# A state-space loop redistributed over the engines: the product with B on GpSimd, the decay in PSUM, the sum over states by accumulating transposes

## The chip, the cores and the metric

The kernel runs on one core of a Trainium2 chip. A core has TensorE (matrix products, PE in the profile; its weight loads are the row PEld), VectorE (DVE), ScalarE (ACT), GpSimd (POOL) and SyncE (SP), which here only issues transfers. They run side by side and wait for each other by semaphores. SBUF is the working memory, PSUM the memory that TensorE writes to; PSUM has eight banks, each of 512 fp32 values per partition. The metric is device time in microseconds for one execution of the whole program, the median of several.

## The reference

The program is two layers of a sequence model with many parts (a conditioned scan, attention, two feed-forward networks, a recurrent network, a mixture of experts). The change touches one part alone, a selective state-space model over 64 sequences of 64 steps and width 256. Its input is the output of the recurrent network. Cut to what matters:

```python
xz = x @ W_in                                # 256 -> 2 * 512
xi, z = jnp.split(xz, 2, axis=-1)
xc = silu(conv4(xi) + b_conv)                # causal, 4 taps, each channel by itself
delta_lr, B, C = jnp.split(xc @ W_xproj, [r, r + n], axis=-1)   # r = 16, n = 16
delta = softplus(delta_lr @ W_dt + b_dt)     # 512 channels
A = -jnp.exp(A_log)                          # 512 x 16
dA  = jnp.exp(delta[..., None] * A)          # decay
dBx = delta[..., None] * B[:, :, None, :] * xc[..., None]
def step(h, inp):                            # along the 64 steps of a sequence
    h = dA_t * h + dBx_t                     # 512 channels x 16 states
    y = einsum('bdn,bn->bd', h, C_t) + D * x_t
    return h, y
...
return y * silu(z) @ W_out
```

For each of the 16 states n the kernel does the same four things with an array of channels by time: an exponential (dA), a product with B's row n, a scan along time, and a product with C's row n. The results are summed over n.

## The kernel before

The 4096 tokens go in 8 chunks of 512 (CH), each 8 whole sequences. The 512 inner channels are four blocks (NI = 4) of 128 partitions. head(c) prepares a chunk in pieces that are interleaved with the states of the chunk before. PSUM is a pool of four banks called ps and four called acc for the whole program. The order in which each engine's instructions stand is set when the program is built.

```python
dAs = [p1.tile([P, NI, CB, L + 1], F32, name=f"dA{i}") for i in range(2)]
hbs = [p1.tile([P, NI, CB, L + 1], F32, name=f"hb{i}") for i in range(3)]
...                                   # column 0 of each sequence is zero, so that the scan restarts
def head(c, v):
    for i in range(NI):
        ps = bank(g)
        for k in range(KD):                                          # L579
            nc.tensor.matmul(ps, w.Win[:, k, ts(i, P)], hs2[:, k, tok], ...)
        acc = v.xc[:, i, :]
        nc.scalar.activation(acc, ps, AF.Identity, bias=..., scale=...)   # L581
        for s in range(1, 4):                                        # L584
            nc.vector.scalar_tensor_tensor(to, seq(ps)[...], taps, to, ALU.mult, ALU.add)
        yield
    nc.scalar.activation(v.xc, v.xc, AF.Silu)
    ...                                   # sz = silu(z): 4 x (two products, one Silu), L592, L593
    ...                                   # dbc = xc @ W_xproj (48 rows: delta_lr, B, C), L597, L598
    for i in range(NI):
        ps = bank(g)
        nc.tensor.matmul(ps, w.Wdt[:, ts(i, P)], v.dbc[:R, :], start=True, stop=True)   # L602
        nc.scalar.activation(z, ps, AF.Identity, bias=...)
        softplus(nc, z, ...)              # 3 on ScalarE, 4 on VectorE (L63 to L69)
        nc.vector.tensor_mul(v.dx[:, i, :], z, v.xc[:, i, :])        # L606
        yield

def broadcast(v, n):                      # rows B_n and C_n onto all 128 partitions
    got = []
    for row in (R + n, R + S + n):
        ps = bank(g)
        nc.tensor.matmul(ps, g.ident[:W, row:row+1].to_broadcast([W, P]), v.dbc, ...)   # L614
        got.append(...)
    return got
...
for c in range(NCH):
    yp = [bank(g, tag="acc") for _ in range(NI)]
    for n in range(S):
        dA, hb = dAs[n % 2], hbs[(c * S + n) % 3]
        for i in range(NI):
            nc.scalar.activation(dA[:, i, :, 1:], seq(now.delta[:, i, :]), AF.Exp, scale=w.A[:, i, n:n+1])  # L629
        nc.vector.tensor_tensor(hv, dx, bc[0], ALU.mult)                        # L634
        nc.vector.tensor_tensor_scan(hf, dA, hf, 0.0, ALU.mult, ALU.add)        # L635
        nc.vector.tensor_tensor(hv, hv, bc[1], ALU.mult)                        # L636
        if n + 1 < S:
            bc = broadcast(now, n + 1)
        for i in range(NI):
            nc.tensor.matmul(yp[i], g.ident, hb[:, i, :, 1:], start=(n == 0), stop=(n == S - 1))   # L640
        next(pieces, None)
    ...
    for i in range(NI):
        nc.vector.scalar_tensor_tensor(xc[:, i, :], xc[:, i, :], D, yp[i], ALU.mult, ALU.add)   # L648
        nc.gpsimd.tensor_mul(xc[:, i, :], xc[:, i, :], now.sz[:, i, :])         # L651
    for k in range(KD):                   # W_out: 4 products each (L655), added to xT (L657)
        ...
```

The scan is one instruction over 4 blocks x 8 sequences x 65 = 2080 elements per partition. The sum over states is four fp32 products with the identity per state (L640), which add up in PSUM. An fp32 product has two records in the trace.

Of the kernel before, what the change touches and what calls it, by code (L numbers as in the profile page):

```python
# [11 lines left out]
F32 = mybir.dt.float32  # L12
BF16 = mybir.dt.bfloat16
AF = mybir.ActivationFunctionType
# [4 lines left out]
P = 128  # L19
# [14 lines left out]
def setup(ctx, tc, a):  # L34

    nc = tc.nc
    g = SimpleNamespace(nc=nc, tc=tc, a=a)
    const = ctx.enter_context(tc.tile_pool(name="const", bufs=1))
    g.psum = ctx.enter_context(tc.tile_pool(name="psum", bufs=4, space=PSUM))
    g.ident = const.tile([P, P], F32, name="ident")  # L40
    make_identity(nc, g.ident)
    g.identb = const.tile([P, P], BF16, name="identb")
    make_identity(nc, g.identb)
    g.xT = const.tile([P, KD, NT], F32, name="xT")
    for k in range(KD):
        nc.sync.dma_start(g.xT[:, k, :], a["xT"][ts(k, P), :])
    g.condT = const.tile([P, KD, B], F32, name="condT")
    nc.sync.dma_start(g.condT, a["condT"].rearrange("(k p) b -> p k b", p=P))
    return g


def bank(g, shape=(P, CH), dt=F32, tag="ps"):
# [500 lines left out]
def mamba(g, w, hs):  # L553
    nc, tc = g.nc, g.tc
    NI, S, R = w.NI, w.S, w.R
    W = R + 2 * S
    nc.scalar.activation(w.A, w.A, AF.Exp)
    nc.vector.tensor_scalar(w.A, w.A, -1.0, None, ALU.mult)
    hs2 = hs.rearrange("p k b t -> p k (b t)")
    seq = lambda t: t.rearrange("p (b l) -> p b l", l=L)  # L560
    with tc.tile_pool(name="m1", bufs=1) as p1, tc.tile_pool(name="m2", bufs=2) as p2:

        dAs = [p1.tile([P, NI, CB, L + 1], F32, name=f"dA{i}") for i in range(2)]
        hbs = [p1.tile([P, NI, CB, L + 1], F32, name=f"hb{i}") for i in range(3)]
        for t in (*dAs, *hbs):
            nc.gpsimd.memset(t[:, :, :, 0:1], 0.0)

        def head(c, v):

            tok = ts(c, CH)  # L570
            v.xc = p2.tile([P, NI, CH], F32, name="xc")
            v.sz = p2.tile([P, NI, CH], F32, name="sz")
            v.delta = p2.tile([P, NI, CH], F32, name="delta")
            v.dx = p2.tile([P, NI, CH], F32, name="dx")
            v.dbc = p2.tile([W, CH], F32, name="dbc")
            for i in range(NI):
                ps = bank(g)
                for k in range(KD):
                    nc.tensor.matmul(ps, w.Win[:, k, ts(i, P)], hs2[:, k, tok], start=(k == 0), stop=(k == KD - 1))  # L579
                acc = v.xc[:, i, :]  # L580
                nc.scalar.activation(acc, ps, AF.Identity, bias=w.col[:, 0, i : i + 1], scale=w.taps[:, i, 3:4])  # L581
                for s in range(1, 4):
                    to = seq(acc)[:, :, s:]
                    nc.vector.scalar_tensor_tensor(  # L584
                        to, seq(ps)[:, :, : L - s], w.taps[:, i, 3 - s : 4 - s], to, ALU.mult, ALU.add
                    )
                yield
            nc.scalar.activation(v.xc, v.xc, AF.Silu)
            for i in range(NI):
                ps = bank(g)  # L590
                for k in range(KD):
                    nc.tensor.matmul(ps, w.Win[:, k, ts(NI + i, P)], hs2[:, k, tok], start=(k == 0), stop=(k == KD - 1))  # L592
                nc.scalar.activation(v.sz[:, i, :], ps, AF.Silu)  # L593
            yield
            ps = bank(g)
            for i in range(NI):
                nc.tensor.matmul(ps[:W, :], w.Wxp[:, i, :], v.xc[:, i, :], start=(i == 0), stop=(i == NI - 1))  # L597
            nc.scalar.copy(v.dbc, ps[:W, :])  # L598
            yield
            for i in range(NI):  # L600
                ps = bank(g)
                nc.tensor.matmul(ps, w.Wdt[:, ts(i, P)], v.dbc[:R, :], start=True, stop=True)  # L602
                z = v.delta[:, i, :]
                nc.scalar.activation(z, ps, AF.Identity, bias=w.col[:, 1, i : i + 1])  # L604
                softplus(nc, z, p2.tile([P, CH], F32, name="t1"), p2.tile([P, CH], F32, name="t2"))
                nc.vector.tensor_mul(v.dx[:, i, :], z, v.xc[:, i, :])  # L606
                yield

        def broadcast(v, n):

            got = []
            for row in (R + n, R + S + n):
                ps = bank(g)
                nc.tensor.matmul(ps, g.ident[:W, row : row + 1].to_broadcast([W, P]), v.dbc, start=True, stop=True)  # L614
                got.append(seq(ps).unsqueeze(1).to_broadcast([P, NI, CB, L]))
            return got

        now = SimpleNamespace()
        for _ in head(0, now):
            pass  # L620
        bc = broadcast(now, 0)
        for c in range(NCH):
            after = SimpleNamespace()
            pieces = head(c + 1, after) if c + 1 < NCH else iter(())
            yp = [bank(g, tag="acc") for _ in range(NI)]
            for n in range(S):
                dA, hb = dAs[n % 2], hbs[(c * S + n) % 3]
                for i in range(NI):
                    nc.scalar.activation(  # L629
                        dA[:, i, :, 1:], seq(now.delta[:, i, :]), AF.Exp, scale=w.A[:, i, n : n + 1]  # L630
                    )
                hv = hb[:, :, :, 1:]
                hf = hb.rearrange("p i b l -> p (i b l)")
                nc.vector.tensor_tensor(hv, now.dx.rearrange("p i (b l) -> p i b l", l=L), bc[0], ALU.mult)  # L634
                nc.vector.tensor_tensor_scan(hf, dA.rearrange("p i b l -> p (i b l)"), hf, 0.0, ALU.mult, ALU.add)  # L635
                nc.vector.tensor_tensor(hv, hv, bc[1], ALU.mult)  # L636
                if n + 1 < S:
                    bc = broadcast(now, n + 1)
                for i in range(NI):
                    nc.tensor.matmul(yp[i], g.ident, hb[:, i, :, 1:], start=(n == 0), stop=(n == S - 1))  # L640
                next(pieces, None)
            for _ in pieces:
                pass
            if c + 1 < NCH:
                bc = broadcast(after, 0)
            xc = now.xc
            for i in range(NI):
                nc.vector.scalar_tensor_tensor(  # L648
                    xc[:, i, :], xc[:, i, :], w.col[:, 2, i : i + 1], yp[i], ALU.mult, ALU.add
                )  # L650
                nc.gpsimd.tensor_mul(xc[:, i, :], xc[:, i, :], now.sz[:, i, :])  # L651
            for k in range(KD):
                ps = bank(g)
                for i in range(NI):
                    nc.tensor.matmul(ps, w.Wout[:, i, ts(k, P)], xc[:, i, :], start=(i == 0), stop=(i == NI - 1))  # L655
                x = g.xT[:, k, ts(c, CH)]
                nc.vector.tensor_add(x, x, ps)  # L657
            now = after
# [446 lines left out]
@with_exitstack  # L1105
def tile_adaln_attn_ffn_d2(ctx: ExitStack, tc: tile.TileContext, a: dict, out: bass.AP):
    g = setup(ctx, tc, a)
    p_mamba, close_mamba = scoped(tc, "w_mamba")
    p_mid, close_mid = scoped(tc, "w_mid")
    p_attn, close_attn = scoped(tc, "w_attn")  # L1110

    w_scan = scan_weights(g, p_attn)
    cs = conditioned_scan(g, w_scan, p_attn)
    w_attn = attention_weights(g, p_attn)
    w_ffn0 = ffn0_weights(g, p_mid)
    w_rnn = rnn_weights(g, p_mid)
    w_mamba = mamba_weights(g, p_mamba)
    rows = regions(g, p_mamba, "ffn1")
    attention(g, w_scan, w_attn, cs)
    close_attn()  # L1120

    ffn0(g, w_ffn0)

    p_hs, close_hs = scoped(tc, "hs", side="right")
    hs = p_hs.tile([P, KD, B, L], F32, name="hs")
    rnn(g, w_rnn, hs)
    close_mid()
    mamba(g, w_mamba, hs)
    close_hs()
    close_mamba()  # L1130

    x2 = ctx.enter_context(tc.tile_pool(name="x2", bufs=1))
    x2T = x2.tile([P, KD, NT], F32, name="x2T")
    routed = ctx.enter_context(tc.tile_pool(name="routed", bufs=1))
    gate = Gate(g, routed, x2T, rows)
    p_moe, close_moe = scoped(tc, "w_moe")
    with tc.tile_pool(name="gate2", bufs=2) as work:
        moe(g, moe_weights(g, p_moe), x2T, lambda c: gate.chunk(c, work))
    close_moe()
    ffn1(g, gate, out)  # L1140


# [76 lines left out]
```

## Time and profile before

| | |
|---|---|
| time, median of 3 | 4410.67 us (4409.87 to 4413.94) |
| span of the profiled execution | 4399.1 us |
| busy PE / VectorE / ScalarE / GpSimd | 3609.5 / 2209.0 / 1187.3 / 195.5 us |
| state-space stage | 1220.6 to 2693.5 us |
| VectorE busy from 1220.6 to 2692 | 1321 of 1471 us |
| largest shares of the chain that ended last | DVE hb L635 10%; PE ps L1044 8%; PE ps L894 8% |

In the page's costliest groups a row reads: line, engine, operation, output <- inputs with partitions x elements, count, then the busy time, the mean of one in ns, and after the second bar the time that the engine was idle just before, with what ended most of that idle time. The granted clock is the share of TensorE's full clock. Several records can overlap, so sums of records can be over the time that they took.

### The profile page before, as it was taken

Reading aid. Unit: us, or ns where it says so; the run is one execution under the profiler, and the core shown is the slowest. Engines: PE = TensorE matmul, PEld = TensorE weight load, DVE = VectorE, ACT = ScalarE, POOL = GpSimd, SP = SyncE. Lnnn points to the kernel's source line nnn. Section 1 sums busy time; section 2 is a strip of 40 time slices with the busy share of each in tenths; the row PEclk is TensorE's granted clock in tenths of the full one; section 3 lists DMA queues with packets and bytes.
Section 4 is the critical chain, followed back from the end, with each engine's and each line's share of the span. In section 5 each row is a group of like instructions: output and inputs, shape, how many; then the busy total and the mean of one; then the engine's idle time right before and its main releaser. Section 6 shows DMA issues by size and latency. Waiting matters only on the chain.

```text
span 4399.1 us, 34313 instructions
## 1 busy us (share of the span) xinstructions
PE 3609.5 (82%) x13521; PEld 1996.3 (45%) x13521; DVE 2209.0 (50%) x2286; ACT 1187.3 (27%) x1967; POOL 195.5 (4%) x247
## 2 busy tenths in 40 slices
PE   3799974549977878778778778999999994999993
PEld 3344432329932322223223225444444444888882
DVE  0355557770069889998898994211111121222223
ACT  0422214432245334244343420111111110111110
POOL 0000000000000000000000000000000001000005
PEclk9899986765578878878788786999999997999995
DMA  9940000000000000000000001000000004555543
GB/s 248 386 169 1 1 1 0 1 0 1 1 0 0 0 0 0 0 0 0 0 0 0 0 0 68 0 4 10 9 10 10 9 9 153 168 171 171 168 141 120
DMA packets 192785, 223.36 MB, mean 51 GB/s; under 512 B 35296, under 2 KB 162080, under 8 KB 192112
## 3 DMA queue, kind: packets, MB, share of 16 engines
q1 hardware_dynamic: 183360, 194.16, 13.9%
q0 software_dynamic: 9264, 27.01, 1.8%
q8 instruction: 106, 1.74, 0.2%
q14 instruction: 55, 0.45, 0.0%
HBM read 131.22 MB, written 89.92 MB: 50 GB/s over the span
## 4 chain that ended last, share of the span: by engine, by line
PE 60%; DVE 27%; issue 5%; ACT 3%; DMA 2%; POOL 1%; SPq 1%; DVEq 0%; POOLq 0%; ACTq 0%
DVE hb L635 10%; PE ps L1044 8%; PE ps L894 8%; PE acc L912 7%; DVE hb L634 5%; PE acc L1065 5%; DVE hb L636 5%; PE acc L279 3%; PE ps L899 3%; PE acc L299 3%; PE acc L640 2%; PE ps L263 2%; PE acc L292 1%; PE acc L827 1%; PE ps L521 1%
## 5 line engine op out<-in xcount | busy, mean ns | idle before, releaser
L640 PE MATMUL acc<-hb,ident 128*128 128x512 f32 x1024 | 630.1, 774 | 254.0 <-DVE hb L636 253.6
L635 DVE TENSOR_TENSOR_SCAN hb<-dA,hb 128x2080 f32<-128x2080 f32 x128 | 572.1, 4482 | 4.2
L640 PEld LDWEIGHTS acc<-hb,ident 128*128 128x128 f32 x1024 | 245.3, 251 | 646.9 <-DVE hb L636 330.6
L629 ACT ACTIVATE dA<-delta,A 128x512 f32<-128x512 f32 x512 | 333.3, 711 | 656.3 <-DVE hb L635 655.6
L1044 PE MATMUL ps<-gxT,w 128*128 128x256 f32 x1560 | 348.5, 383 | 0.9 <-issue 0.9
L1049 DVE TENSOR_TENSOR gh<-gs,ps 128x256 f32<-128x256 f32 x195 | 82.1, 421 | 473.3 <-ACT gs L1048 473.3
L1044 PEld LDWEIGHTS ps<-gxT,w 128*128 128x128 f32 x1560 | 294.2, 191 | 52.5 <-issue 13.8
L614 PE MATMUL ps<-dbc,ident 48*128 48x512 f32 x512 | 271.8, 648 | 51.9 <-ACT delta L604 29.6
L634 DVE TENSOR_TENSOR hb<-dx,ps 128x2048 f32<-128x2048 f32 x128 | 290.2, 2280 | 21.8 <-PE ps L614 21.7
L906 DVE TENSOR_TENSOR h<-act,acc 128x512 f32<-128x512 f32 x128 | 88.0, 688 | 412.7 <-ACT act L903 211.3
L636 DVE TENSOR_TENSOR hb<-hb,ps 128x2048 f32<-128x2048 f32 x128 | 290.3, 2279 | 5.1
L894 PE MATMUL ps<-xT,moe_r 128*128 128x512 f32 x512 | 240.6, 592 | 0.0
L912 PE MATMUL acc<-h,moe_r 128*128 128x512 f32 x512 | 239.4, 592 | 0.0
L1065 PE MATMUL acc<-w,gh 128*128 128x256 f32 x936 | 231.3, 392 | 0.0
L903 ACT ACTIVATE act<-ps 128x512 f32<-128x512 f32 x128 | 76.4, 597 | 423.5 <-PE ps L894 423.5
L1065 PEld LDWEIGHTS acc<-w,gh 128*128 128x128 f32 x936 | 165.0, 189 | 55.0 <-issue 38.8
L614 PEld LDWEIGHTS ps<-dbc,ident 48*128 48x128 f32 x512 | 87.5, 193 | 220.6 <-issue 137.7
L584 DVE SCALAR_TENSOR_TENSOR xc<-ps,taps,xc 128x504 f32<-128x504 f32 (+2 forms) x96 | 68.3, 723 | 226.2 <-ACT xc L581 226.0
L901 DVE SCALAR_TENSOR_TENSOR h<-ps,act 128x512 f32<-128x512 f32 x64 | 44.2, 691 | 256.8 <-PE ps L899 256.8
L1048 ACT ACTIVATE gs<-ps 128x256 f32<-128x256 f32 x195 | 74.9, 384 | 320.6 <-PE ps L1044 320.6
L894 PEld LDWEIGHTS ps<-xT,moe_r 128*128 128x128 f32 x512 | 97.3, 190 | 122.4 <-issue 122.4
L469 PE MATMUL ps<-identb,q 128*128 128x128 bf16 x256 | 27.9, 275 | 149.6 <-DVE q L412 149.6
(309 smaller groups left out, 4818.2 us busy)
## 6 DMA issues: line engine op xcount, KB each, us to landing
w<-in_ffn_W_dram SPq DMA_DIRECT2D x117, 640.0 KB, 4.7
ffn_x<-zero SPq DMA_DIRECT2D x32, 1024.0 KB, 10.7
ffn_y<-zero SPq DMA_DIRECT2D x32, 1024.0 KB, 10.7
gx<-ffn_x SPq DMA_DIRECT2D x39, 256.0 KB, 4.5
ffn_y<-gy POOLq DMA_DIRECT2D x39, 256.0 KB, 4.5
w<-in_ffn_W_dram SPq DMA_DIRECT2D x117, 64.0 KB, 4.3
xT<-in_xT_dram SPq DMA_DIRECT2D x2, 2048.0 KB, 10.5
T<-in_cond_pad_dram SPq DMA_DIRECT2D x2, 2048.0 KB, 22.1
```

What stands on the lines that cost most here:

```text
L279: nc.tensor.matmul(ps, y[:, k, ts(pr, P)], wa.Wv[:, k, ts(hg, 8 * V)], start=(k == 0), stop=(k == KD - 1))
L299: nc.tensor.matmul(ps, wa.Wout[:, i, ts(k, P)], oT[:, i, :], start=(i == 0), stop=(i == H // 2 - 1))
L614: nc.tensor.matmul(ps, g.ident[:W, row : row + 1].to_broadcast([W, P]), v.dbc, start=True, stop=True)
L629: nc.scalar.activation(dA[:, i, :, 1:], seq(now.delta[:, i, :]), AF.Exp, scale=w.A[:, i, n : n + 1])
L634: nc.vector.tensor_tensor(hv, now.dx.rearrange("p i (b l) -> p i b l", l=L), bc[0], ALU.mult)
L635: nc.vector.tensor_tensor_scan(hf, dA.rearrange("p i b l -> p (i b l)"), hf, 0.0, ALU.mult, ALU.add)
L636: nc.vector.tensor_tensor(hv, hv, bc[1], ALU.mult)
L640: nc.tensor.matmul(yp[i], g.ident, hb[:, i, :, 1:], start=(n == 0), stop=(n == S - 1))
L894: nc.tensor.matmul(ps, lhs[:, k, ts(j, P)], x[:, k, :], start=(k == 0), stop=(k == KD - 1))
L912: nc.tensor.matmul(po[k], lhs[:, j, ts(k, P)], h, start=(i == 0), stop=(i == total - 1))
L1044: nc.tensor.matmul(ps[:, j, :], v.w12[:, k, ts(j * full + i, P)], v.xT[:, k, :], start=(k == 0), stop=(k == KD - 1))
L1065: nc.tensor.matmul(po[:, s, :], v.h[r, i, ts(s, P)], v.w3[r, i, :], start=(i == 0), stop=(i == full))
```

## The change

Work is moved off VectorE. The product with B (L634) goes to GpSimd[...]; so B's rows are no longer spread by TensorE but written to DRAM and read back with a partition broadcast, four states at a time. The decay dA moves from SBUF to PSUM, so that the scan reads only one operand from SBUF. C's rows are still spread by TensorE, but in bf16: each fp32 value is split into three bf16 parts, which lie at partitions 0, 32 and 64 of one tile, and one bf16 product with a selecting column adds them up. The sum over states is no longer a product with the identity as the weights but a transpose, which adds up in PSUM with hb as the weights; what it sums is transposed, so it is copied to SBUF and transposed back once per half chunk. As the eight PSUM banks now hold dA (4), the sums (2), C (1) and all other products (1), a step handles two of the four channel blocks, and a chunk is two rounds of 16 states. Two of the softplus' operations go to GpSimd, and the softplus' ScalarE operations are batched by function. The general PSUM pool is closed before the stage and opened again after it. The core of the diff, with cuts marked:

```diff
-    with tc.tile_pool(name="m1", bufs=1) as p1, tc.tile_pool(name="m2", bufs=2) as p2:
-        dAs = [p1.tile([P, NI, CB, L + 1], F32, name=f"dA{i}") for i in range(2)]
-        hbs = [p1.tile([P, NI, CB, L + 1], F32, name=f"hb{i}") for i in range(3)]
+        tc.tile_pool(name="m3", bufs=3) as p3,
+        tc.tile_pool(name="mps", bufs=1, space=PSUM) as pp,
+    ):
+        one = lambda: pp.tile([P, CH], F32, name="mp")
+        dAs = [pp.tile([P, PI, CB, L], F32, name=f"dA{i}") for i in range(2)]
...
+        rows = 2 * 32 + S
+        parts = [p1.tile([rows, CH], BF16, name=f"parts{i}") for i in range(2)]
...
             for i in range(NI):
-                ps = bank(g)
+                ps = one()
...                                         # the same for every product of the head
+            v.B = tc.dram_tile((S, CH), F32, name=f"B{c}")
+            nc.sync.dma_start(v.B, v.dbc[R : R + S, :])
...                                         # C in three bf16 parts: 3 copies on ScalarE, 2 subtractions on VectorE
-                softplus(nc, z, p2.tile([P, CH], F32, name="t1"), p2.tile([P, CH], F32, name="t2"))
-                nc.vector.tensor_mul(v.dx[:, i, :], z, v.xc[:, i, :])
...                                         # Abs, one Exp and one Ln over all four blocks; 3 on VectorE per block
+                nc.gpsimd.tensor_sub(z, z, v.dx[:, i, :])
+                nc.gpsimd.tensor_mul(v.dx[:, i, :], z, v.xc[:, i, :])
...
+        def spread_b(v, n):
+            t = p3.tile([P, NB, CH], F32, name="Bn")            # NB = 4
+            nc.sync.dma_start(t, v.B[n : n + NB, :].partition_broadcast(P))
+            return t
...
-            yp = [bank(g, tag="acc") for _ in range(NI)]
-            for n in range(S):
+            for i0 in range(0, NI, PI):                          # PI = 2
+                yp = [pp.tile([P, CH // P, P], F32, name=f"yp{i}") for i in range(PI)]
+                for n in range(S):
+                    if n % NB == 0:
+                        Bn = spread_b(now, n)
+                    dA = dAs[step % 2]
...
+                    hb = p3.tile([P, PI, CH], F32, name="hb")
+                    nc.gpsimd.tensor_mul(hb, now.dx[:, i0 : i0 + PI, :], Bn[:, n % NB, :]...)
+                    cb = pp.tile([P, CH], F32, name="cb")
+                    nc.tensor.matmul(cb, pick[:, n : n + 1].to_broadcast([rows, P]), now.parts, start=True, stop=True)
-                nc.vector.tensor_tensor(hv, now.dx.rearrange("p i (b l) -> p i b l", l=L), bc[0], ALU.mult)
-                nc.vector.tensor_tensor_scan(hf, dA.rearrange("p i b l -> p (i b l)"), hf, 0.0, ALU.mult, ALU.add)
-                nc.vector.tensor_tensor(hv, hv, bc[1], ALU.mult)
-                for i in range(NI):
-                    nc.tensor.matmul(yp[i], g.ident, hb[:, i, :, 1:], start=(n == 0), stop=(n == S - 1))
+                    nc.vector.tensor_tensor_scan(hf, dA.rearrange("p i b l -> p (i b l)"), hf, 0.0, ALU.mult, ALU.add)
+                    nc.vector.tensor_tensor(hb, hb, cb.unsqueeze(1).to_broadcast([P, PI, CH]), ALU.mult)
+                    for i in range(PI):
+                        for t in range(CH // P):
+                            nc.tensor.matmul(yp[i][:, t, :], hb[:, i, ts(t, P)], g.ident,
+                                start=(n == 0 and t == 0), stop=(n == S - 1 and t == CH // P - 1),
+                                is_transpose=True, skip_group_check=True)
+                    if i0 == 0 and n == 2:
+                        gates(c, now)                            # sz = silu(z), moved out of head
+                    elif i0 or n > 3:
+                        next(pieces, None)
+                for i in range(PI):
+                    yT = p2.tile([P, CH // P, P], F32, name="yT")
+                    nc.scalar.copy(yT, yp[i])
+                    ps = one()
+                    for t in range(CH // P):
+                        nc.tensor.transpose(ps[:, ts(t, P)], yT[:, t, :], g.ident)
+                    ...                                          # + D * xc on VectorE, * sz on GpSimd, as before
```

## The prediction

> **What bounds the kernel now.** I first read the page's list of costliest groups, to find which stage the change touches, then the rows in time order at its two ends, then the busy times by stage, and last the order of waits. The changed loop is the state-space stage. Its first product (line 579) starts at 1220.6 us, its first scan (line 635) at 1270.2, and its last add (line 657) ends at 2693.5. So it takes 1473 us of the 4399 us span: 50 us of a first head that nothing hides, seven chunks of 181 us (the chunk-end product of line 655 comes back at 1631.9, 1812.8 and 1994.0) and about 156 us for the last chunk. The rest, 2926 us, is not touched.
>
> ```profile
> L640 PE MATMUL acc<-hb,ident 128*128 128x512 f32 x1024 | 630.1, 774 | 254.0 <-DVE hb L636 253.6
> L635 DVE TENSOR_TENSOR_SCAN hb<-dA,hb 128x2080 f32<-128x2080 f32 x128 | 572.1, 4482 | 4.2
> L629 ACT ACTIVATE dA<-delta,A 128x512 f32<-128x512 f32 x512 | 333.3, 711 | 656.3 <-DVE hb L635 655.6
> L614 PE MATMUL ps<-dbc,ident 48*128 48x512 f32 x512 | 271.8, 648 | 51.9 <-ACT delta L604 29.6 <-DVE hb L636 19.9 <-DVE xc L584 2.3
> L634 DVE TENSOR_TENSOR hb<-dx,ps 128x2048 f32<-128x2048 f32 x128 | 290.2, 2280 | 21.8 <-PE ps L614 21.7
> L636 DVE TENSOR_TENSOR hb<-hb,ps 128x2048 f32<-128x2048 f32 x128 | 290.3, 2279 | 5.1
> ```
>
> The reader should see the last column: the scan and the two products wait 31 us in all, while ScalarE (line 629) and TensorE (line 640) wait hundreds of microseconds for VectorE. By stage, where the columns after the length are busy PE, weight loads, VectorE, ScalarE and GpSimd, then the granted clock:
>
> ```profile
> 1812.00:1994.00 182.00, 142.03 (x258) 52.68 (x256) 165.11 (x86) 73.19 (x102) 5.79 (x5) 0.81 0.00 0
> 1100.00:1220.00 120.00, 120.00 (x565) 120.00 (x564) 0.00 (x0) 26.52 (x71) 0.00 (x0) 0.50 0.00 1
> ```
>
> One chunk: VectorE 165 of 182 us, GpSimd 6. VectorE bounds the stage, at 16 x (2.28 + 4.48 + 2.28) = 145 us for the states and some 25 us for the next chunk's head. The second line is the recurrent stage just before: TensorE is busy the whole time and still has a clock of 0.50. I come back to that.
>
> **What the skill says.** "SBUF — State Buffer", section "Who interferes with whom": VectorE and GpSimd share a pair of ports under an exclusive lock; a VectorE instruction with two SBUF inputs contends with a GpSimd instruction that reads SBUF, one with at most one SBUF input does not. That is why the decay goes to PSUM. The trace agrees as far as it reaches: at 1809.05 three GpSimd products run back to back in 3.72 us (1.24 each, as elsewhere) while VectorE runs line 648, whose second input is PSUM. No run yet shows them beside a scan. "GPSIMD Engine Reference", section 3.1, gives 4497 ns for a product-like operation on 2048 fp32; the trace's 1267 ns for 512 (line 651) fits that slope. "TensorE: Matmul & The Clock Gate", Part 4, says that transposes do not count as busy for the clock in the same way. The trace shows the two rates:
>
> ```profile
> 129.00 2.11 PE L167 MATMUL acc<-ident,cv 128*128 128x128 f32 x16
> 3684.37 1.09 PE L1033 MATMUL ps<-ident,gx 128*128 128x128 f32 x4 [53.94 <-DMA gx<-ffn_x]
> ```
>
> Sixteen fp32 transposes among dense products end after 2.11 us, so, with 0.27 for the length of one, they are (2.11 - 0.27) / 15 = 0.12 us apart. Four after a pause take 1.09, the first of them 0.45, so they are 0.21 apart. I call these warm and cold.
>
> **The change part by part.** A step now handles half the inner channels (1024 elements per partition), so a chunk has 32 steps instead of 16.
>
> VectorE: the product with B goes. The scan's slope is (4482 - 149) / 2080 = 2.08 ns per element, so 1024 elements take 2.13 + 0.15 = 2.29 us. The product with C takes 1024 x 1.04 + 0.15 = 1.21 us. Independent neighbours overlap by 0.08 us (scan at 1885.68 for 4.49, next at 1890.28 if dependent; 1892.48 for 2.28, next at 1894.68 if not). The built order puts the scan of step s+1 before the product of step s, so a step costs 2.21 + 1.13 = 3.35 us. A chunk: 32 x 3.35 = 107, plus the conv (12 x 0.72), softplus (about 4 x 1.8) and end (6 x 0.72), 20: 127 us against 165. VectorE alone would save 38 us per chunk, 300 in all.
>
> GpSimd: a product of 1024 takes (1267 - 140) x 2 + 140 = 2.4 us, 32 of them 77 us, plus 12 of 1.27 for softplus and gate, 15: 92 us per chunk. It is not the bound by its sum.
>
> TensorE: per step the old identity products (half of 8 records and half of 4, 0.59 us each warm) become eight transposes and one bf16 product for C. Cold that is 0.2 + 7 x 0.21 + 0.42 = 2.1 us for the transposes and about 0.5 for C. The head's fp32 products stay: 64 records a chunk.
>
> ScalarE: two exponentials of 504 per step, 1.4 us at most, 32 of them 45 us a chunk; it had 73 us busy. The decay has two buffers, so it runs a step ahead.
>
> But the step is a ring. hb has three buffers, so GpSimd may fill step s+3 only after the transposes of s have read it. Follow one buffer from the end of product s: transposes 2.15 with the wake-up, GpSimd 2.4 + 0.15 for two hand-overs, scan 2.29 - 0.08, product s+2 (which stands after scan s+3) 1.21. That is 8.1 us for two steps: 4.0 us per step cold; warm it is 7.2 / 2 = 3.6. Both are above VectorE's 3.35. Cold or warm? Eight transposes and C stream 8 x 128 + 512 = 1536 columns per 4 us, a third of the 4800 cycles that the cold 1.2 GHz of the same page's Part 1 gives; and the recurrent stage stayed at 0.50 although TensorE was never idle there[...]. So I expect cold between the head's products, with a mean of about 0.65. 32 x 4.0 = 128 us.
>
> What the ring does not hide: TensorE is idle 4.0 - 2.4 = 1.6 us per step. Eight groups of four records (conv and gate) take 3.0 us at 0.75 us per record, 1.4 too long each: 11. The product for B, C and the step width, eight records: 6 - 1.6 = 4. The two output products stand in the order before the next chunk's second and third transposes, the first of them waits for the last gate product on GpSimd, and both take the one spare bank: 12. Bursts of four softplus operations on GpSimd, 5.1 us against 1.6 idle: 3. VectorE's inserted pieces where they stand between scan and product: 4. Half-way change of the sum banks: 3. Sum 37. One chunk 165 us, against 181.
>
> At the ends: the first head has one bank instead of four, so each conv piece goes product, ScalarE, three VectorE operations in series, 6.3 x 4 = 25 us against some 14; with the softplus' last steps on GpSimd (8 x 1.27 = 10) I take 72 us against 50. The last chunk has no next head: 128 + 2 + 20 for copies, transposes back and outputs through one bank = 150 against 156.
>
> Sum: 72 + 7 x 165 + 150 = 1377, against 1473. Saved 96 us: 4411 - 96 = 4315.
>
> **Rivals.** (a) VectorE stays the bound: clock high, ring slack. Per chunk 127 + about 18 of stalls at the ends = 145; stage 72 + 1015 + 145 = 1232, time 4170. For it: the head's products could warm the clock, as in the stage before (0.81). Against: the ring's 3.6 even when warm. (b) TensorE in the loop: a cold clock throughout and head products that fall between transposes and the C product. Then 64 records at 1.22 instead of 0.75 add 30 us, and a chunk is 185 to 195; time 4455 to 4525. For it: single banks for C and for the head make every product a round trip. (c) The port lock bites after all (a scan from PSUM is not exempt): 3.35 + 2.4 = 5.75 per step, 184 plus stalls, 205 a chunk; about 4600. The trace at 1809 speaks against it, for one operation. (d) B's way through DRAM: 1 MB per four steps. A like transfer (1024 KB, the zero fill) lands in 10.7 us, four steps are 16 us and there are three buffers, so it is hidden except once in the first head; a few microseconds.
>
> **Range and chances.** The ring term is firm to about 0.3 us per step, 10 us a chunk, 75 in all; the stall terms sum to 37 a chunk and are likelier too large than too small, as stalls on two engines overlap. Low 4200, a little above (a); high 4430, towards (b). Two per cent faster is 4322, just above my centre, so faster 0.50, within 0.38, slower 0.12.
>
> **What would show each step.** In the changed profile: the scan about 2.3 us and the GpSimd product about 2.4, neither stretched (if either is bimodal, (c)); the scan's idle before it put down to GpSimd, and GpSimd's to TensorE, about 0.6 and 1.6 us per step (the ring); a granted clock of 0.55 to 0.7 in the loop (0.8 or more speaks for (a)); transposes 0.21 us apart; TensorE waits at the chunk ends on GpSimd. I am wrong if VectorE is over 90% busy in a chunk, if the product with C waits mostly for the C bank, or if the untouched 2926 us move.

## The result, and the profile after

| | before | after |
|---|---|---|
| time, median (4 runs each, side by side) | 4412.31 us | 4312.6 us (4310.83 to 4315.02) |
| ratio, 95% interval | 1 | 0.9774 [0.9757, 0.9791] |
| state-space stage | 1473 us | 1376 us (1219.8 to 2595.9) |
| its first head, one chunk | 50, 181 us | 70, 166.1 us |

The change makes the program 2.3% faster. By the two profiles the stage is 97 us shorter. (A chunk is counted from the first output add, line 726 here, to that of the next chunk, as the mean of six.) What comes after the stage takes 1713 us, and 1706 before. That difference doesn't come from the change: over all runs below this part takes 1712 to 1716 us where the kernel before, timed beside them, took 4411 to 4412 us, and 1702 to 1706 where it took 4402; the execution of the kernel before that was profiled took 4401 us.

The rows of the loop in the page's costliest groups of the changed kernel, with line, engine, operation, output <- inputs, then busy time and mean in ns, then the idle time before:

```profile
L696 PE MATMUL yp<-ident,hb 128*128 128x128 f32 x2048 | 417.7, 368 | 418.3 <-DVE hb L692 418.3
L685 POOL TENSOR_TENSOR hb<-dx,Bn 128x1024 f32<-128x1024 f32 x256 | 603.4, 2359 | 488.8 <-PE yp L696 488.8
L691 DVE TENSOR_TENSOR_SCAN hb<-dA,hb 128x1024 f32<-128x1024 f32 x256 | 584.7, 2287 | 172.5 <-POOL hb L685 151.1
...
L681 ACT ACTIVATE dA<-delta,A 128x504 f32<-128x504 f32 x512 | 348.6, 683 | 524.2 <-DVE hb L691 514.8
...
L692 DVE TENSOR_TENSOR hb<-hb,cb 128x1024 f32<-128x1024 f32 x256 | 309.0, 1207 | 42.5 <-PE cb L689 41.6
```

Read the last column from row to row: TensorE's transposes wait for VectorE's product, GpSimd waits for the transposes, the scan waits for GpSimd. Before, the scan and the two products waited 31 us in all, now the scan alone waits 172. No single engine is the bound any more; a loop of waits is. Most of one chunk, with the columns of the stage view as before:

```profile
1784.00:1948.00 164.00, 100.18 (x365) 58.91 (x366) 132.39 (x95) 77.37 (x102) 89.92 (x45) 0.68 0.14 52
```

VectorE is busy 132 of 164 us (81%; it was 91%), GpSimd 90, and the granted clock fell from 0.81 to 0.68. The loop itself, in the chain of waits over a quiet stretch, that is, steps in the second half of a chunk beside which no piece of a head runs (start, length, what the chain went through):

```profile
1762.83 1.20 DVE hb L692
1764.03 0.04 issue
1764.07 1.98 PE yp L696 x8
1766.05 0.07 issue
1766.12 2.36 POOL hb L685
1768.48 0.02 issue
1768.51 0.04 DVE hb L691
1768.54 2.16 issue
1770.70 0.02 DVEq L691
1770.72 1.20 DVE hb L692
```

The ten lines are one turn: product with C, transposes, GpSimd's product, scan (the 0.04 and the 2.16 put down to "issue" are its 2.29, less the overlap), product with C. From product to product it is 1770.72 - 1762.83 = 7.89 us, and the turn is worth two steps: 3.95 us per step. VectorE's own work in those two steps is 2 x 3.31.

### The profile page after: what moved, and what is told of

It is laid out like the page before. It is cut to its first block, busy times and chain, and to the rows that moved or that the text cites. A ratio compares the mean times of both kernels' runs of the same rounds, so it can differ in the third digit from the quotient of the medians.

```text
span 4308.9 us, 37088 instructions
## 1 busy us (share of the span) xinstructions
PE 3315.8 (77%) x14402; PEld 2063.8 (48%) x14417; DVE 1961.0 (46%) x2371; ACT 1234.4 (29%) x1977; POOL 891.1 (21%) x565
## 4 chain that ended last, share of the span: by engine, by line
PE 64%; DVE 14%; POOL 8%; issue 6%; ACT 5%; DMA 2%; SPq 1%; another core or an unknown queue 0%; POOLq 0%; DVEq 0%; ACTq 0%
PE ps L1113 8%; PE ps L963 8%; PE acc L981 8%; PE acc L1134 5%; POOL hb L685 5%; PE yp L696 4%; DVE hb L691 4%; DVE hb L692 3%; PE acc L285 3%; PE ps L968 3%; PE acc L305 3%; PE mp L604 2%; PE ps L269 2%; PE acc L298 1%; PE acc L896 1%
## 5 line engine op out<-in xcount | busy, mean ns | idle before, releaser
L696 PE MATMUL yp<-ident,hb 128*128 128x128 f32 x2048 | 417.7, 368 | 418.3 <-DVE hb L692 418.3
L685 POOL TENSOR_TENSOR hb<-dx,Bn 128x1024 f32<-128x1024 f32 x256 | 603.4, 2359 | 488.8 <-PE yp L696 488.8
L691 DVE TENSOR_TENSOR_SCAN hb<-dA,hb 128x1024 f32<-128x1024 f32 x256 | 584.7, 2287 | 172.5 <-POOL hb L685 151.1
L696 PEld LDWEIGHTS yp<-ident,hb 128*128 128x128 f32 x2048 | 337.1, 192 | 600.0 <-DVE hb L692 547.0
L681 ACT ACTIVATE dA<-delta,A 128x504 f32<-128x504 f32 x512 | 348.6, 683 | 524.2 <-DVE hb L691 514.8
L692 DVE TENSOR_TENSOR hb<-hb,cb 128x1024 f32<-128x1024 f32 x256 | 309.0, 1207 | 42.5 <-PE cb L689 41.6
L820 POOL DMA_INDIRECT ffn_x<-rows,row x64 | 61.6, 962 | 839.8 <-DVE row L813 724.1
L1137 POOL DMA_DIRECT2D ffn_y<-gy x39 | 27.9, 716 | 609.2 <-ACT gy L1136 592.0
L604 PE MATMUL mp<-hs,Win 128*128 128x512 f32 x128 | 103.8, 958 | 55.4 <-ACT dA L681 40.9
```

Of the source, the lines that this page charges most:

```text
L681: nc.scalar.activation(dA[:, i, :, 1:], seq(now.delta[:, i0 + i, :])[:, :, 1:], AF.Exp, scale=w.A[:, i0 + i, n : n + 1])
L685: nc.gpsimd.tensor_mul(hb, now.dx[:, i0 : i0 + PI, :], Bn[:, n % NB, :].unsqueeze(1).to_broadcast([P, PI, CH]))
L692: nc.vector.tensor_tensor(hb, hb, cb.unsqueeze(1).to_broadcast([P, PI, CH]), ALU.mult)
L696: nc.tensor.matmul(yp[i][:, t, :], hb[:, i, ts(t, P)], g.ident, start=(n == 0 and t == 0), stop=(n == S - 1 and t == CH // P - 1), is_tran ...
```

## The experiments

Each group was timed beside the kernel before, so ratios to it are compared.

| run | what differs from the changed kernel | ratio, 95% interval | us |
|---|---|---|---|
| (changed kernel) | | 0.9774 [0.9757, 0.9791] | 4312.6 |
| e1_hb4 | four hb buffers | 0.9783 [0.9766, 0.9799] | 4315.8 |
| e3_decay_sbuf | decay in SBUF | 1.0150 [1.0133, 1.0167] | 4478.5 |
| e4_identity | sum by identity products | 1.0118 [1.0101, 1.0135] | 4462.7 |
| e5_b_vector | product with B on VectorE | 0.9956 [0.9940, 0.9973] | 4393.1 |
| e6a_order_hb3 | no scan ahead, three buffers | 0.9765 [0.9749, 0.9781] | 4299.3 |
| e6b_order_hb4 | one scan ahead, four buffers | 0.9675 [0.9659, 0.9691] | 4259.0 |
| e7_cbfirst | e6b, and C before the transposes | 0.9402 [0.9387, 0.9418] | 4138.9 |
| e8_no_head | heads left out | 0.930 (one run) | 4094.2 |
| e9a_cbfirst_hb3 | C before the transposes | 0.9584 [0.9568, 0.9600] | 4227.8 |
| e9b_cbfirst_hb4 | e9a, four buffers | 0.9480 [0.9465, 0.9496] | 4183.1 |
| e9c_cbfirst_hb5 | e9a, five buffers | 0.9371 [0.9356, 0.9387] | 4135.6 |

**e1_hb4: one more buffer.**

```diff
-                    hb = p3.tile([P, PI, CH], F32, name="hb")
+                    hb = p3.tile([P, PI, CH], F32, name="hb", bufs=4)
```

> One size alone: hb gets four buffers instead of three. Ring theory (the step is set by product with C, transposes, GpSimd product, scan, product, for two steps with three buffers): the ring then spans three steps, 7.9 / 3 = 2.6 us, and stops binding. What binds next is the single bank for C: product with C 1.21, transposes issued 1.8, C's product 0.63, hand-overs 0.1, together 3.7 us instead of 3.95 per step. In the quiet half of a chunk scans start 3.7 apart, the scan no longer waits for GpSimd, the product with C waits for TensorE's C row; time 4245 to 4275. Rival A (VectorE's own work, 3.35 per step, and stalls by other engines set the step, and three buffers are enough): the same within 10 us of 4313.

Nothing came of it, as the rival had said; but not for the rival's reason. VectorE in the same stretch (rows in time order: start, length, engine, line, what; in brackets the idle time before and its releaser):

```profile
1758.72 2.29 DVE L691 TENSOR_TENSOR_SCAN hb<-dA,hb 128x1024 f32<-128x1024 f32 x1 [0.79 <-POOL hb L685]
1760.93 1.20 DVE L692 TENSOR_TENSOR hb<-hb,cb 128x1024 f32<-128x1024 f32 x1
1762.42 2.29 DVE L691 TENSOR_TENSOR_SCAN hb<-dA,hb 128x1024 f32<-128x1024 f32 x1 [0.30 <-POOL hb L685]
1764.63 1.20 DVE L692 TENSOR_TENSOR hb<-hb,cb 128x1024 f32<-128x1024 f32 x1
1766.62 2.29 DVE L691 TENSOR_TENSOR_SCAN hb<-dA,hb 128x1024 f32<-128x1024 f32 x1 [0.79 <-POOL hb L685]
```

Two steps take 7.90 us and the scan still waits for GpSimd. The order that was built explains it. Counted over VectorE's instructions of the whole loop, in the changed kernel one scan stands ahead of the product in 207 of the 256 steps; with four buffers two scans do, in 198 of them.

With three buffers the scan is thus mostly one step ahead of the product, with four it is two. The number of steps in a turn of the ring is the buffers less the lead of the scan: 3 - 1 = 2, and 4 - 2 = 2 again. The added buffer was spent on order. My expectation had left the order out.

**e3_decay_sbuf: the decay back in SBUF.**

```diff
-        dAs = [pp.tile([P, PI, CB, L], F32, name=f"dA{i}") for i in range(2)]
+        dAs = [p1.tile([P, PI, CB, L], F32, name=f"dA{i}") for i in range(2)]
```

> One part undone: the decay lies in SBUF, everything else as in the changed kernel. Port theory: the scan then has two SBUF inputs and excludes the GpSimd product, so that each step holds both in a row, 2.29 + 2.36 = 4.65 us or more instead of 3.95; some of the scans or GpSimd products are stretched to up to 4.6 us; time 4313 + 256 x 0.7 to 1.0 = 4490 to 4570. Rival B (no lock for a scan, PSUM is only a matter of space): both durations stay at 2.29 and 2.36 and the time within 10 us of 4313.

The ratio is 1.0150: the kernel would be 1.5% slower than before. The instructions of the two lines over the whole run (durations in ns, least / median / greatest):

```profile
L691 DVE TENSOR_TENSOR_SCAN hb<-dA,hb x256: 2258/2292/4422, 1291.7 to 2738.0; 128x1024 f32<-128x1024 f32 x128
...
L685 POOL TENSOR_TENSOR hb<-dx,Bn x256: 2333/3129/4352, 1289.3 to 2734.5; 128x1024 f32<-128x1024 f32 x128
```

A scan of up to 4.42 us is 2.29 plus most of a GpSimd product, and GpSimd's median is 3.13 instead of 2.35. With the decay in PSUM the same two lines read 2257/2290/2294 and 2336/2353/2877. The port theory holds: with both its inputs in SBUF the scan and GpSimd's product stretch each other, with one in PSUM they don't. In a quiet stretch the scan keeps its 2.29 us, GpSimd's product takes 3.41, and the scan waits 1.07 for it, so that a step is 4.48 us (scans at 1830.80 and 1835.28) and not the 4.65 or more that I had expected. The time is 11 us under my range. Placing the decay in PSUM is worth 166 us, more than the whole change.

**e4_identity: the sum over states as before.**

```diff
-                        for t in range(CH // P):
-                            nc.tensor.matmul(yp[i][:, t, :], hb[:, i, ts(t, P)], g.ident, ..., is_transpose=True, ...)
+                        nc.tensor.matmul(yp[i], g.ident, hb[:, i, :], start=(n == 0), stop=(n == S - 1))
...                                     # and yp used directly at the end: no copy, no transposes back
```

> One part undone: the sum over states by fp32 products with the identity as weights, two per step, instead of eight transposes; no copy and no transposes back at the end of a half chunk. Ring theory: four records of 0.6 (warm) to 1.2 us take the place of 2.0 us of transposes, about 2.6 to 3.2 at the clock near 0.8 that long products earn, so the ring is 4.25 to 4.5 us per step, and TensorE's own sum, 32 x 3.4 + 48 = 157 us per chunk, is near the bound: 4380 to 4450. Rival C (transposes are not on the path): 4313 within 10. Rival D (the cold clock of the transposes costs more than they save, as the head's products would run warm): below 4300.

4463 us, 13 over the range. In the groups of its stage, GpSimd's wait for the sum grew from 489 to 689 us, and the products that take the transposes' place are as long per record as before:

```profile
L695 PE MATMUL yp<-hb,ident 128*128 128x512 f32 x1024 | 651.2, 765 | 363.1 <-DVE hb L692 362.5
L685 POOL TENSOR_TENSOR hb<-dx,Bn 128x1024 f32<-128x1024 f32 x256 | 606.1, 2368 | 698.3 <-PE yp L695 688.9 <-DVE xc L609 4.7 <-DVE hb L691 4.7
```

Undoing this part costs 150 us, so the transposes are on the path and rival C is out. How much of the 150 is the ring is not shown. In some quiet steps four of these products take 1.98 us, as long as the eight transposes, and two steps take 7.91 us (scans at 1799.87 and 1807.78); in others they take 3.3 us. The product's wait for C's row over the stage grew too, from 42 to 160 us. The clock rose (0.81 in the chunk from 1672 to 1853 against 0.68, and 0.847 over the program against 0.81), which did not pay.

**e5_b_vector: the product with B back on VectorE.**

```diff
-                    nc.gpsimd.tensor_mul(
+                    nc.vector.tensor_mul(
                         hb, now.dx[:, i0 : i0 + PI, :], Bn[:, n % NB, :]...)
```

> One part undone: the product with B back on VectorE (B still spread by DMA, operands in SBUF), the decay in PSUM and the transposes kept. VectorE's step is 2.21 + 1.13 + 1.13 = 4.5 us and becomes the bound again: 32 x 4.5 = 143 plus 20 to 25 for the head and some 8 of stalls at the ends, 172 to 178 us per chunk against 164: 4380 to 4430. If the time stays within 10 us of 4313, VectorE was not what the change relieved.

4393, in the range. The scan's idle time is gone and VectorE is busy for 168 of a chunk's 175 us, so it is the bound again, and the product takes 1.28 us there:

```profile
L691 DVE TENSOR_TENSOR_SCAN hb<-dA,hb 128x1024 f32<-128x1024 f32 x256 | 583.0, 2282 | 4.2 <-ACT dA L681 0.2
...
L685 DVE TENSOR_TENSOR hb<-dx,Bn 128x1024 f32<-128x1024 f32 x256 | 326.1, 1279 | 10.0 <-PE yp L696 5.8 <-POOL dx L649 3.6
```

By the change VectorE was relieved of 326 us and the program gained 80: the rest went into waits, the ring's among them.

**e6a and e6b: VectorE's order held.** The scan's start value is read from the product k steps back (k = 1 in e6a, 2 in e6b). The first decay of a tile is zero, so the value changes nothing but the order. e6b has four buffers too.

```diff
-  nc.vector.tensor_tensor_scan(hf, dA.rearrange("p i b l -> p (i b l)"), hf, 0.0, ALU.mult, ALU.add)
+  nc.vector.tensor_tensor_scan(hf, dA..., hf, done[-k][:, 1, CH - 1 : CH] if len(done) >= k else 0.0, ALU.mult, ALU.add)
   nc.vector.tensor_tensor(hb, hb, cb..., ALU.mult)
+  done.append(hb)
```

> Only VectorE's order is changed, with three buffers as before: the scan of step s+1 takes its start value from the product with C of step s (the first decay is zero, so the value changes nothing), so that it can't stand before that product. In the run with four buffers the order built put two scans ahead instead of one, so the ring stayed at two steps; here it is product, transposes, GpSimd, scan, product over three steps, 7.9 / 3 = 2.6 us, although there is no further buffer. Ring-and-order theory: the next bounds are VectorE itself without overlap (2.29 + 1.21 + 0.1 = 3.6) and the single C bank (3.7); scans 3.7 apart in the quiet half, time 4245 to 4275. Rival (the slack between scan and product is needed to hide waits, the order as built is the best): same or slower than 4313.

> Four buffers, and the order held at one scan ahead: the scan of step s+2 takes its start value from the product of step s. Ring over three steps, VectorE overlaps (3.35), the C bank (3.7) binds: scans 3.7 apart, 4240 to 4270, and the product with C, not the scan, is what waits. If four buffers do nothing even so, the ring was not the limit: 4313.

e6a missed: ratio 0.9765, no change. Its quiet step did shorten, to 3.81 us (scans at 1756.31 and 1760.12), but every instruction now waits for the one before it on its own engine (a scan of 2.35, 0.10 to the product, 1.22, 0.14 to the next scan), and the 36 us of 256 x 0.14 did not show in the end. They were lost outside the quiet stretch. Where is shown in part: with no scan ahead in any of the 256 steps, the scan's wait for GpSimd over the run fell from 151 to 31 us, but the product's wait for C's row rose from 42 to 77. e6b, with at most one scan ahead, behaved as expected, with 4259 us:

```profile
1757.68 2.35 DVE L692 TENSOR_TENSOR_SCAN hb<-dA,hb 128x1024 f32<-128x1024 f32 x1
1760.03 1.22 DVE L693 TENSOR_TENSOR hb<-hb,cb 128x1024 f32<-128x1024 f32 x1
1761.39 2.35 DVE L692 TENSOR_TENSOR_SCAN hb<-dA,hb 128x1024 f32<-128x1024 f32 x1
1763.75 1.22 DVE L693 TENSOR_TENSOR hb<-hb,cb 128x1024 f32<-128x1024 f32 x1
```

Scans are 3.71 apart. The scan's rows have no wait for GpSimd here any more; over the run it is 31 us. Which bound this is the step alone doesn't tell, since VectorE's own work without the overlap lies only 0.1 us below the C bank's loop (3.6 in e7, where C's row comes early). With the fourth buffer kept for the ring, the same buffer that did nothing in e1 pays 1.1% (0.9675 against 0.9783).

**e7_cbfirst: C's row before the transposes**, on top of e6b.

```diff
-                    cb = pp.tile([P, CH], F32, name="cb")
-                    nc.tensor.matmul(cb, pick[:, n : n + 1].to_broadcast([rows, P]), now.parts, ...)
+                    cb = ahead or spread_c(now, n)          # spread_c: the same tile and product
...
                     nc.vector.tensor_tensor(hb, hb, cb..., ALU.mult)
+                    ahead = spread_c(now, (n + 1) % S) if n + 1 < S or i0 + PI < NI else None
                     ...                                     # then the eight transposes
```

> As the run before (four buffers, one scan ahead), and C's row for step s+1 is issued before the transposes of step s instead of after them. The C bank's loop is then 1.21 + 0.7 and free, the transposes come 0.45 later, which the three-step ring (8.4 / 3 = 2.8) bears. VectorE's 3.35 to 3.4 is the bound: scans 3.4 apart, time 4312 minus up to 256 x 0.55 = 140, less where head pieces interrupt: 4170 to 4220. If the C bank wasn't the second limit: as the run before.

The gain was larger than I had expected (0.9402, which is 0.962 of the changed kernel, where 0.967 to 0.979 was said), and by another route: the quiet step is 3.6, not 3.4 (scans at 1716.28, 1719.88, 1723.47), because the start value costs the overlap, and the chunk fell further than the quiet steps account for. A chunk is 143.4 us, and VectorE is busy for 136.5 us of the second and 136.9 of the third. What a chunk takes beyond 32 quiet steps fell from 40 to 28 us.

**e8_no_head.**

```diff
-            pieces = head(c + 1, after) if c + 1 < NCH else iter(())
+            pieces = iter(())
...
-            now = after
```

> Leaves out the head of every chunk after the first (all chunks use the first one's), the output products and gates stay. By the sum of the prediction the head's pieces cost 11 / 2 (conv) + 4 (the product for B, C and step width) + 3 (GpSimd bursts) + 4 (VectorE pieces) + 3 of the half-way change in part, about 18 to 20 us per chunk, 7 times: a chunk of 144 to 147 instead of 164, time 4170 to 4190. If the head is hidden in the ring's idle times: above 4250.

It leaves out seven of eight heads, so the chunks after the first compute with the first one's values. The chunk is 136.6 us, 7 to 10 below what I had expected: the heads cost 30 us per chunk (166.1 - 136.6) and what is left beside the quiet steps (32 x 3.95 = 126.4) only 10.

**e9a, e9b, e9c: C first without the start value**, with three, four and five buffers (the edit of e7's second part, and bufs=4 or 5).

> Only C's place is changed: its row for step s+1 stands before the transposes of step s; three buffers, no start value from another tile. Ring theory: the ring is still two steps and now holds C's product too (about 0.4 more): 8.3 / 2 = 4.15 us per quiet step, slower there, 256 x 0.2 = 51 us, so about 4350 (ratio 0.985), less what the freed C bank saves around the head's pieces. Rival (the C bank was the limit all along, the ring follows from it): below 4250 (ratio under 0.965).

> C first and four buffers, without the start value that held VectorE's order. The order built stays mostly one scan ahead, so the ring is over three steps; neighbours on VectorE are independent again and overlap: 3.35 to 3.4 us per quiet step instead of the 3.6 of the run with the start value. 256 x 0.2 = 50 us at most below that run (ratio 0.940), so a ratio of 0.928 to 0.938. If the start value cost nothing: 0.940.

> As the run before with five buffers. In quiet steps VectorE is the bound already, so nothing there; the fifth buffer only helps where a head piece or a burst on GpSimd holds the ring: 0 to 20 us less (ratio 0.924 to 0.938).

e9a is the sharpest test of the ring and of my sum at once. In the quiet stretch:

```profile
1739.08 2.29 DVE L696 TENSOR_TENSOR_SCAN hb<-dA,hb 128x1024 f32<-128x1024 f32 x1 [1.50 <-POOL hb L691]
1741.28 1.20 DVE L697 TENSOR_TENSOR hb<-hb,cb 128x1024 f32<-128x1024 f32 x1
1742.39 2.28 DVE L696 TENSOR_TENSOR_SCAN hb<-dA,hb 128x1024 f32<-128x1024 f32 x1
1744.59 1.20 DVE L697 TENSOR_TENSOR hb<-hb,cb 128x1024 f32<-128x1024 f32 x1
1747.29 2.29 DVE L696 TENSOR_TENSOR_SCAN hb<-dA,hb 128x1024 f32<-128x1024 f32 x1 [1.50 <-POOL hb L691]
```

Two steps take 8.21 us, 4.1 each: the quiet step got slower by what the ring says (4.15 expected). Yet the run is 1.9% faster than the changed kernel. Its chunk is 153.6 us instead of 166.1, so the rest of the chunk got some 17 us shorter. My reading is that where head pieces stand on TensorE, C's row came late, behind a piece and eight transposes. The product's wait for C's row over the stage supports it in part, 9 us against 42; the scan's wait for GpSimd also fell, from 151 to 94. But the edit changed the built order as well: a scan stands ahead of the product in 123 of the 256 steps, against 220 in the changed kernel. Order alone gained nothing in e6a; how the 17 us divide between C's place and the order is open. The rival that I had named (the C bank is the limit all along) is wrong for the quiet steps and may be right for the disturbed ones.

e9b missed its range (0.9480): the quiet step is 3.31, about as expected, but a chunk of 150.0 us has 44 us beyond its quiet steps, where e7 has 28; why is not shown. e9c, with five buffers, takes part of that back: 0.9371, at the edge of its range, with a chunk of 143.2 us. It has the lowest ratio of the full versions, just under e7's: 6.3% under the kernel before and 4.1% under the change. Scan and product wait some 34 us each in the whole stage:

```profile
L696 DVE TENSOR_TENSOR_SCAN hb<-dA,hb 128x1024 f32<-128x1024 f32 x256 | 579.3, 2283 | 33.6 <-POOL hb L691 29.5 <-ACT dA L687 3.8
...
L697 DVE TENSOR_TENSOR hb<-hb,cb 128x1024 f32<-128x1024 f32 x256 | 309.9, 1210 | 33.7 <-PE cb L671 32.2
```

The scan's idle time fell from 172 us to 34.

## Why the prediction was right, step by step

- **The time**: 4312.6 measured, 4315 predicted; the stage 1376 against 1377. That closeness is luck in part, as the ends and the stall terms show.
- **Durations**: scan 2287 ns (2.29 us), product with C 1207 (1.21), GpSimd's product 2359 (2.4), transposes 1.97 from first start to last end (2.1). All were worked out from the profile before.
- **The ring, 4.0 us per step cold**: 3.95 measured, and shown as the cause: e6b lengthens the turn to three steps and the step falls to the next bound named beforehand (3.71 for 3.7), e9a puts C's product into the turn, which grows from 7.89 to 8.21 us, and the step rises to 4.1. The rival that VectorE stays the bound (a) is out: 81% busy, 3.31 of 3.95 us. So are the lock (c), with both durations unstretched, and B's way through DRAM (d): no wait for it is among the scan's or GpSimd's releasers.
- **Cold clock**: a quiet stretch of the changed kernel has a granted clock of 0.50, the chunk 0.68, where 0.65 was expected. The working was off: TensorE is busy for 17.9 of the 36 us below, half and not the third that I had got from its columns. Whether the clock stays low because these are transposes or because TensorE is half idle, no run separates.

```profile
1745.00:1781.00 36.00, 17.90 (x69) 13.06 (x70) 27.66 (x17) 10.96 (x16) 22.66 (x11) 0.50 0.15 58
```

- **Stalls, 37 us per chunk**: 40 measured (166.1 - 126.4), but badly divided. By e8 the heads cost 30; I had given them some 18 (conv 5.5, the product for B, C and step width 4, GpSimd bursts 3, VectorE pieces 4, and part of the half-way change). Gates, output products and the rest cost 10 where I had 19; before the output products, for which alone I had 12 per chunk, TensorE is idle for only 7 us in the whole run (line 724). I had taken head pieces as a loss only by their length over TensorE's idle time; that C's row also stood behind them, I had named in rival (b) but not put into the sum. e9a, which moves C's row, gains 12 us per chunk net, a changed order included.
- **Ends**: first head 70 us (72). The first chunk, up to the second chunk's first scan, takes 155 (165), the last one, from its first scan on, 155 (150).

## What to carry to other kernels

Where several engines pass one tile around, write down the turn: the durations on every engine between two uses of a buffer, divided by the buffers less the lead of the engine that runs ahead. Where that number is above the busiest engine's sum and above every other loop of waits, here that of the single C bank, it is the step. Look at the order that was built before adding a buffer, since the order can spend it, and put small products that another engine waits for ahead of long ones in TensorE's queue.

## What the runs showed of the hardware that I had not expected

The exclusion between VectorE and GpSimd is visible in the changed kernel too, in the softplus, where VectorE reads two tiles in SBUF. Line 642 there, over the run:

```profile
L642 DVE SCALAR_TENSOR_TENSOR dx<-t,dx x32: 676/680/2824, 1271.4 to 2392.4; 128x512 f32<-128x512 f32 x32
```

It takes 680 ns alone and up to 2824, which is 680 plus most of a 2.35 us product on GpSimd; its mean is 1187. At 1723.53, for one, two of them take 3.42 us, while GpSimd runs a product from 1723.30 on for 2.51. The one-input operation before it (line 641) is stretched as well, up to 1495 ns and 778 in the mean, where its like took 422 in the kernel before. I had put these waits at nothing; over the run they add up to some 28 us of VectorE (32 x 0.51 + 32 x 0.36). For line 641 the prediction said too much: the Trainium skill, "SBUF — State Buffer", section "Who interferes with whom", exempts a VectorE instruction with at most one SBUF input only outside the two-port performance modes, a condition that I had left out. Whether line 641 runs in such a mode no run here shows.
